# Swapping the order of two kinds of attention scores inside a half step of a four-layer network

## The chip, the cores and the metric

The program runs on one core of a Trainium2 chip. One core has a matrix engine (TensorE, in the profile PE, its weight loads PEld), a vector engine (VectorE, DVE), a scalar engine (ScalarE, ACT), GpSimd (POOL), and SyncE (SP), which here only issues DMAs. Each engine works through its own queue of instructions in order and waits on semaphores for the others. The metric is the device time of one execution in microseconds; lower is better.

## The reference

A network of four layers works on `x` of shape (8, 512, 128). In every layer `x` is normalised, and an attention part and a feed-forward part are added to it:

```python
xn = _layernorm(x, axis=-1)
x = x + _L0_attn_ref(xn, ...) + _L0_ffn_ref(xn, ...)
...
x = x + _L3_attn_ref(xn, ...) + _L3_ffn_ref(xn, ...)
```

Layers 0, 2 and 3 have softmax attention with 16 heads of 8 channels; the change touches only these. Layer 0 masks keys behind the query:

```python
scores = jnp.einsum('bhqd,bhkd->bhqk', qc, k) * scale
causal_mask = k_pos[None, :] > q_pos[:, None]
scores = jnp.where(causal_mask[None, None], -jnp.inf, scores)
...
p = jax.nn.softmax(scores - m, axis=-1)
oc = jnp.einsum('bhqk,bhkd->bhqd', p, v)
```

Layer 2 multiplies the scores by a lower triangular mask and subtracts a million times its complement, and layer 3 adds a bias that depends on the distance of query and key, without a mask. Layer 1 has a linear attention with decay. The feed-forward parts are mixtures of experts of several kinds.

## The kernel before, in words

The three softmax layers share the function `attention`. A unit of work is one batch element `b` and one group `g` of four heads. The scores of a unit are made twice. The straight scores (tile `s`, queries on the partitions) serve only to find the maximum of each row: `first` makes the products (line 297), `first_rest` adds the causal mask as a product with an identity (line 312, layers 0 and 2) and lets VectorE take the maximum (line 318; in layer 3 line 325 besides, for blocks with a near bias). The transposed scores (tile `t`, keys on the partitions) serve for the softmax itself: `second` makes the products (line 366) and adds the negated maximum, which is spread over the partitions by a product with `pick` (line 376, the picks). `second_rest` adds the bias of layer 3 (line 394) or the mask of layer 0 (line 400), and ScalarE takes the exponential (line 404). In layer 2 GpSimd then clears the masked part (line 408). `weigh` multiplies the exponentials with the values (line 421), and `finish` and `divide` complete a unit.

A unit is cut into half steps, 6 in the causal layers and 8 in layer 3. A half step holds two heads of a kind and one or two blocks of keys. The heads of a group lie in the four quarters of 32 rows of the partitions. In half step `x` the straight scores are those of the pair `1 - x % 2` and the transposed ones those of the pair `x % 2`, so that the two kinds use different quarters of the array's rows:

```python
pr = 1 - x % 2                  # first
pr = x % 2                      # second
r = 32 * (2 * pr + k)
```

The straight scores run five units ahead of the transposed ones (`AHEAD`), since the maximum must be known for a whole batch element before it is subtracted. Both kinds, and some tiles of the feed-forward parts, take their place in PSUM from one ring of three buffers:

```python
return ps.tile([P, 2, T], F32, tag="pair", name=name, bufs=3)
```

A buffer comes free when its reader is done: the maximum on VectorE for straight scores, the exponential on ScalarE for transposed ones. Which of the three buffers a tile takes is settled when the program is built.

The function `run` writes out the order of TensorE's queue by hand, inside `tc.manual_schedule`. In each half step it calls `first`, `second`, `first_rest` and `second_rest`, then `now`, which inserts the tasks due at that place (projections, transposes, work of the feed-forward parts), and after every second half step `weigh`. A unit's last block is weighed in the second half step of the unit that follows. The other engines' queues follow from this order and from the builder's own plan.

Of the kernel before, what the change touches and what calls it, by code (L numbers as in the profile page):

```python
# [36 lines left out]
def blk(i, n=P):  # L37
    return slice(i * n, (i + 1) * n)
# [3 lines left out]
def network(ctx: ExitStack, tc: tile.TileContext, io: dict):  # L42
# [11 lines left out]
    def ps_pair(name):  # L54
        return ps.tile([P, 2, T], F32, tag="pair", name=name, bufs=3)
# [12 lines left out]
    x = []  # L68
# [120 lines left out]
    def attention(L, w, causal, scale, bias=None, soft=None, vpad=None, add_masks=False):  # L189
# [9 lines left out]
        st = {}  # L199
# [23 lines left out]
        def spans(x, straight):  # L223

            out, c = [], 0
            for j in pieces[x]:
                n = T - j * P if causal else T
                if straight and (causal or bias is not None):
                    j = NI - 1 - j
                out.append((j, c, n))  # L230
                c += n
            return out, c
# [125 lines left out]
        def second(b, g, x):  # L358

            pr = x % 2  # L360
            q, key, mT = st[b]["q", g], st[b]["k", g], st[b]["mT"]
            s = st["t"] = ps_pair(f"t{L}_{b}_{g}_{x}")
            for k in range(2):
                r = 32 * (2 * pr + k)
                for j, c, n in spans(x, False)[0]:
                    nc.tensor.matmul(  # L366
                        s[:, k, c : c + n],
                        lhsT=key[r : r + 32, blk(j)],
                        rhs=q[r : r + 32, T - n : T],
                        start=(c == 0),  # L370
                        stop=False,
                    )
            for k in range(2):
                r = 32 * (2 * pr + k)
                for j, c, n in spans(x, False)[0]:
                    nc.tensor.matmul(  # L376
                        s[:, k, c : c + n],
                        lhsT=pick[r : r + 32, 2 * pr + k, g : g + 1].to_broadcast([32, P]),
                        rhs=mT[r : r + 32, T - n : T],
                        start=False,  # L380
                        stop=(j == pieces[x][-1] and not add_masks and not (bias is not None and j >= 2)),
                    )

        def second_rest(b, g, x):
            pr = x % 2
            s = st.pop("t")
            blocks, width = spans(x, False)
            if bias is not None and pieces[x][0] >= 2:
                (j,) = pieces[x]
                for k in range(2):  # L390
                    h = g * HG + 2 * pr + k
                    n = 128 * (j - 1)
                    for part in range(2):
                        nc.tensor.matmul(  # L394
                            s[:, k, :n], lhsT=bias[2], rhs=bias[1](h)[part][:, 256 - n :], start=False, stop=part == 1
                        )
            if add_masks:
                for j, c, n in blocks:
                    for k in range(2):
                        nc.tensor.matmul(  # L400
                            s[:, k, c : c + P], lhsT=ident_bf, rhs=mask_kq, start=False, stop=(j == pieces[x][-1])
                        )
            p = wk.tile([P, 2, T], F32, tag="p", name=f"p{L}_{b}_{g}_{x}", bufs=4)
            nc.scalar.activation(p[:, :, :width], s[:, :, :width], AF.Exp, scale=scale)  # L404
            if causal and not add_masks:

                for j, c, n in blocks:
                    nc.gpsimd.affine_select(  # L408
                        p[:, :, c : c + P], p[:, :, c : c + P], pattern=[[0, 2], [1, P]], compare_op=ALU.is_ge,
                        fill=0.0, base=0, channel_multiplier=-1,  # L410
                    )
            for j, c, n in blocks:
                st[b, g, j, pr] = p[:, :, c : c + n]
# [83 lines left out]
    def usual(at, A, start, soft, norms=True):  # L497

        end = A.nh
        for b in range(NB):  # L500
            u = start + 4 * b
            if start + b >= 2:
                at(u - 8, -4, A.begin, b, not norms)
                if norms:
                    at(u - 8, 0, A.normed_turned, b)
                at(u - 8, 2, A.project, b)
                at(u - 4, 3, A.values, b)
                if soft:
                    at(u - 3, 3, A.behind, b)
            if start + b >= 1:  # L510
                at(u - 1, 0, A.maxima, b)
                at(u - 1, 3, A.turn_maxima, b)
            for g in range(NG):
                at(u + g + 1, 2, A.finish, b, g)
                at(u + g + 1, 4, A.divide, b, g)
            at(u + 5, 0, A.end, b)
            at(u + 5, 2, A.add, b)

    def run(layers, tasks, soft, normed=None, begun=0):

        units = [(A, b, g) for A in layers for b in range(NB) for g in range(NG)]
        where = [0]
        for A, _, _ in units:
            where.append(where[-1] + A.nh)
        todo = {}

        def at(u, x, f, *args):

            n = len(units)
            t = (layers[0].nh * u if u < 0 else where[u] if u <= n else where[n] + layers[-1].nh * (u - n)) + x  # L530
            todo.setdefault(t, []).append((f, args))

        for k, A in enumerate(layers):
            usual(at, A, k * NB * NG, soft[k], normed is None)
        tasks(at)
        A = layers[0]

        def now(t):
            for f, args in todo.pop(t, []):
                f(*args)  # L540

        with tc.manual_schedule(engines={mybir.EngineType.PE}):
            for b in range(begun, 2):
                A.begin(b)
                turn_norm(A.L, b, A.st[b]["xn"])
                if normed is not None:
                    normed(b, A.st[b]["xn"])
                A.project(b)
                if b == 0:
                    for g in range(NG):  # L550
                        A.load(0, g)
            for u in range(AHEAD):
                _, b, g = units[u]
                for x in range(A.nh):
                    if x % 2 == 0:
                        pairs = [A.first(b, g, x), A.first(b, g, x + 1)]
                    A.first_rest(b, g, x, pairs[x % 2])
                    if u == 1 and x == 0:
                        A.values(0)
                    if u == 1 and x == 3:  # L560
                        A.values(1)
                    if soft[0] and u in (2, 3) and x == 3:
                        A.behind(u - 2)
                    now((u - AHEAD) * A.nh + x)
                if u < 2:
                    A.load(1, u)
            A.maxima(0)
            A.turn_maxima(0)
            for u, (A, b, g) in enumerate(units):
                F, fb, fg = units[u + AHEAD] if u + AHEAD < len(units) else (None, 0, 0)  # L570
                if u + AHEAD + 1 < len(units):
                    N, nb, ng = units[u + AHEAD + 1]
                    N.load(nb, ng)
                done = 0
                for x in range(A.nh):
                    firsts = []
                    if F:
                        upto = -(-(x + 1) * F.nh // A.nh)
                        firsts, done = range(done, upto), upto
                    for y in firsts[:-1]:  # L580
                        F.first_rest(fb, fg, y, F.first(fb, fg, y))
                    if firsts:
                        s = F.first(fb, fg, firsts[-1])
                    A.second(b, g, x)
                    if firsts:
                        F.first_rest(fb, fg, firsts[-1], s)
                    A.second_rest(b, g, x)
                    now(where[u] + x)
                    back, blocks = A.weights.get(x, (0, ()))
                    if u >= back:  # L590
                        B, wb, wg = units[u - back]
                        for j in B.weights[1][1] if back else blocks:
                            B.weigh(wb, wg, j)
            for j in A.weights[1][1]:
                A.weigh(b, g, j)
            for t in sorted(todo):
                now(t)
# [822 lines left out]
    def more23(at):  # L1420
# [5 lines left out]
        for b in range(NB):  # L1426
# [15 lines left out]
            at(u + 5, 2, store, b)  # L1442

    run([layer2, layer3], more23, [True, False], begun=2)


# [87 lines left out]
```

## Time and profile before

| | |
|---|---|
| median of 3 runs | 2989.63 us (2984.65 to 3001.01) |
| the profiled execution | 2772.28 us, its span 2770.6 us |
| mean granted TensorE clock in it | 0.896 |
| TensorE busy | 2455.6 us, 89% of the span |
| VectorE busy | 1602.8 us, 58% |
| ScalarE busy | 1227.3 us, 44% |
| GpSimd busy | 590.8 us, 21% |

The profiled execution is shorter than the runs without a profile; durations below are those of the profiled one. The four layers follow each other: layer 0 up to about 830 us, layer 1 to about 1580 us, then layers 2 and 3 in one schedule, with layer 3 from about 2200 us.

In the groups of the profile a row gives the line, engine, operation, what is written and read, and the count, then the busy time and the mean duration of one in ns, then the engine's idle time in front of these instructions and what ended most of it. In the timeline a row begins with start and duration. Ends of matrix products are modelled, so starts are the better guide. A row of waits gives the total in us, the number of times and the longest.

### The profile page before, as it was taken

How to read it: one execution, taken by the hardware profiler on the slowest of the kernel's cores; microseconds unless marked ns; L12 is line 12 of the kernel's file. 1: busy time of each engine (PE TensorE's matmuls, PEld its weight loads, DVE VectorE, ACT ScalarE, POOL GpSimd, SP SyncE). 2: the span in 40 equal slices, each digit the busy share in tenths (PEclk: the TensorE clock that was granted, in tenths of full speed). 3: DMA queues.
4: the chain of work that ended last, by engine and by line, in shares of the span. 5: the costliest groups of instructions: out<-in, count | busy, mean ns of one | idle time of the engine just before them, and what ended most of it. 6: DMA issues, size and time to landing. Idle time of an engine off the chain costs nothing.

```text
span 2770.6 us, 45233 instructions
## 1 busy us (share of the span) xinstructions
PE 2455.6 (89%) x17158; PEld 1553.5 (56%) x17158; DVE 1602.8 (58%) x3966; ACT 1227.3 (44%) x1779; POOL 590.8 (21%) x931
## 2 busy tenths in 40 slices
PE   5889988898887899999998788888888899999999
PEld 3555566777773566778886644444443344444444
DVE  8774542222222488756666656666566677777670
ACT  1433456566563333222222044444454455555556
POOL 2027720000005165500002133323332200000000
PEclk6877899999996788999999689889897899999899
DMA  7443346555541221222222322222122111222200
GB/s 221 155 144 124 126 129 180 169 171 165 165 124 39 69 52 48 77 82 80 81 86 61 102 66 67 75 82 65 55 63 63 51 46 58 69 66 65 67 24 10
DMA packets 170792, 252.38 MB, mean 91 GB/s; under 512 B 21712, under 2 KB 94672, under 8 KB 170320
## 3 DMA queue, kind: packets, MB, share of 16 engines
q1 hardware_dynamic: 157904, 221.40, 25.9%
q0 software_dynamic: 12672, 28.10, 3.5%
q8 instruction: 136, 2.23, 0.3%
q14 instruction: 80, 0.66, 0.1%
HBM read 155.57 MB, written 93.85 MB: 90 GB/s over the span
## 4 chain that ended last, share of the span: by engine, by line
PE 39%; DVE 11%; ACT 3%; POOL 2%; issue 2%; DMA 2%; SPq 0%; POOLq 0%; ACTq 0%; DVEq 0%
PE o L421 6%; DVE max L318 6%; PE s L297 4%; PE t L366 3%; PE o L1084 3%; PE rc L1293 3%; PE t L376 2%; PE t L394 2%; PE p L237 2%; PE y L786 2%; PE s L1061 1%; PE h L999 1%; PE h L1001 1%; ACT p L404 1%; DVE sum L325 1%
## 5 line engine op out<-in xcount | busy, mean ns | idle before, releaser
L318 DVE TENSOR_REDUCE max<-s 128x2 f32<-128x1024 f32 (+3 forms) x768 | 664.3, 885 | 376.3 <-PE s L312 268.9
L404 ACT ACTIVATE p<-t 128x1024 f32<-128x1024 f32 (+1 forms) x640 | 596.5, 938 | 548.3 <-PE t L400 195.4
L366 PE MATMUL t<-q,k 32*128 32x512 f32 (+3 forms) x1536 | 326.8, 453 | 109.3 <-ACT p L404 72.4
L297 PE MATMUL s<-k,q 32*128 32x512 f32 (+3 forms) x1536 | 319.0, 452 | 47.4 <-DVE max L318 26.4
L421 PE MATMUL o<-p,vpad 128*32 128x512 f32 (+3 forms) x3072 | 352.2, 547 | 5.0 <-DVE vpad L256 2.5
L800 POOL DMA_INDIRECT yk<-ys_d,slots x160 | 162.0, 1013 | 880.7 <-DMA ys_d<-y 740.0
L297 PEld LDWEIGHTS s<-k,q 32*128 32x128 f32 x1536 | 142.7, 201 | 335.4 <-issue 179.4
L376 PE MATMUL t<-mT,pick 32*128 32x512 f32 (+3 forms) x1536 | 265.8, 371 | 0.0
L366 PEld LDWEIGHTS t<-q,k 32*128 32x128 f32 x1536 | 147.9, 202 | 202.8 <-ACT p L404 101.7
L786 PE MATMUL y<-wt,h 128*128 128x128 f32 x1632 | 202.5, 278 | 17.6 <-DVE xsT L775 11.5
L786 PEld LDWEIGHTS y<-wt,h 128*128 128x128 f32 x1632 | 191.5, 192 | 27.4 <-ACT h L890 10.6
L752 POOL DMA_INDIRECT xs_d<-xr,slots x160 | 157.7, 985 | 160.0 <-DVE slots L744 108.5
L1084 PEld LDWEIGHTS o<-v,a 128*128 128x128 f32 x1280 | 158.7, 199 | 28.0 <-issue 23.8
L888 PE MATMUL h<-xsT,wt 128*128 128x256 f32 x632 | 152.8, 385 | 18.0 <-DVE xsT L775 13.3
L408 POOL TENSOR_SCALAR_AFFINE_SELECT p<-p 128x256 f32<-128x256 f32 x256 | 102.4, 414 | 296.9 <-ACT p L404 295.8
L1084 PE MATMUL o<-v,a 128*128 128x65 f32 x1280 | 163.3, 282 | 1.3 <-DVE a L1071 1.3
L376 PEld LDWEIGHTS t<-mT,pick 32*128 32x128 f32 x1536 | 153.5, 211 | 1.2 <-ACT mT L355 0.9
L890 ACT ACTIVATE h<-h,wt 128x256 f32<-128x256 f32 x316 | 121.8, 478 | 58.7 <-issue 55.5
L421 PEld LDWEIGHTS o<-p,vpad 128*32 128x32 f32 x3072 | 71.3, 114 | 129.7 <-issue 99.9
L888 PEld LDWEIGHTS h<-xsT,wt 128*128 128x128 f32 x632 | 113.8, 190 | 37.7 <-DVE xsT L775 19.2
L312 PE MATMUL s<-mask_qk,ident_bf 128*128 128x128 bf16 x1024 | 133.9, 245 | 0.0
L895 DVE TENSOR_TENSOR y<-y,wt 128x256 f32<-128x256 f32 x79 | 33.5, 424 | 162.4 <-PE y L786 150.7
(271 smaller groups left out, 3655.8 us busy)
## 6 DMA issues: line engine op xcount, KB each, us to landing
wt<-in_f_w SPq DMA_DIRECT2D x79, 578.0 KB, 4.1
q<-apartq SPq DMA_DIRECT2D x96, 256.0 KB, 2.7
k<-apartk SPq DMA_DIRECT2D x96, 256.0 KB, 3.0
wt<-in_f_w SPq DMA_DIRECT2D x23, 768.0 KB, 5.3
xs<-xs_d SPq DMA_DIRECT2D x102, 128.0 KB, 3.3
ys_d<-y SPq DMA_DIRECT2D x102, 128.0 KB, 4.1
xs_d<-zero SPq DMA_DIRECT2D x50, 256.0 KB, 3.9
apartq<-highq SPq DMA_DIRECT2D x48, 256.0 KB, 3.0
```

Source lines behind the costliest of these rows:

```text
L297: nc.tensor.matmul(s[:, j, c : c + n], lhsT=q[r : r + 32, blk(i)], rhs=k[r : r + 32, :n], start=(c == 0), stop=not causal,)
L312: nc.tensor.matmul(s[:, j, c + n - P : c + n], lhsT=ident_bf, rhs=mask_qk, start=False, stop=(i == spans(x, True)[0][-1][0]),)
L318: anchor["vector"] = nc.vector.tensor_reduce(m[:, i, g, 2 * pr : 2 * pr + 2], s[:, :, c : c + n - e], AX.X, ALU.max, negate=True).ins
L366: nc.tensor.matmul(s[:, k, c : c + n], lhsT=key[r : r + 32, blk(j)], rhs=q[r : r + 32, T - n : T], start=(c == 0), stop=False,)
L376: nc.tensor.matmul(s[:, k, c : c + n], lhsT=pick[r : r + 32, 2 * pr + k, g : g + 1].to_broadcast([32, P]), rhs=mT[r : r + 32, T - n : T], ...
L404: nc.scalar.activation(p[:, :, :width], s[:, :, :width], AF.Exp, scale=scale)
L421: nc.tensor.matmul(st[b, g][blk(h, 32), T - n : T], lhsT=vpad[b % 2][:, j, g * HG + h, :], rhs=st[b, g, j, h // 2][:, h % 2, :], start=(j ...
L752: ins = nc.gpsimd.indirect_dma_start(out=xs_d, out_offset=bass.IndirectOffsetOnAxis(ap=slots[:, b * NI + i, k : k + 1], axis=0), in_=state ...
L786: nc.tensor.matmul(py[:, blk(k)], lhsT=h[:, f, blk(k)], rhs=out(wt)[:, f, :], start=(f == 0), stop=(f == 3))
L800: nc.gpsimd.indirect_dma_start(out=yk[:, k, :], out_offset=None, in_=ys_d, in_offset=bass.IndirectOffsetOnAxis(ap=slots[:, b * NI + i, k : ...
L888: nc.tensor.matmul(s[:, f, :], lhsT=wt[:, blk(f)], rhs=xsT, start=True, stop=True)
L1084: nc.tensor.matmul(o[:, k, i * 65 : i * 65 + 65], lhsT=lin[b, c, "a", j][:, k, blk(i - j)], rhs=v1[b % 2][:, j, 2 * c + k, :], start=(j == ...
```

## The change

In `run`, `second` now comes before `first`, and `second_rest` before `first_rest`. The picks of line 376 move from `second` to the start of `second_rest`. So TensorE's order within a half step was straight products, transposed products, picks, mask of the straight scores, bias or mask of the transposed ones; it becomes transposed products, straight products, picks, bias or mask of the transposed scores, mask of the straight ones. The instructions themselves are the same.

```diff
         def second(b, g, x):
 
             pr = x % 2
-            q, key, mT = st[b]["q", g], st[b]["k", g], st[b]["mT"]
+            q, key = st[b]["q", g], st[b]["k", g]
             s = st["t"] = ps_pair(f"t{L}_{b}_{g}_{x}")
...
+
+        def second_rest(b, g, x):
+            pr = x % 2
+            s, mT = st.pop("t"), st[b]["mT"]
+            blocks, width = spans(x, False)
             for k in range(2):
                 r = 32 * (2 * pr + k)
-                for j, c, n in spans(x, False)[0]:
+                for j, c, n in blocks:
                     nc.tensor.matmul(
                         s[:, k, c : c + n],
                         lhsT=pick[r : r + 32, 2 * pr + k, g : g + 1].to_broadcast([32, P]),
...
-
-        def second_rest(b, g, x):
-            pr = x % 2
-            s = st.pop("t")
-            blocks, width = spans(x, False)
...
                     for y in firsts[:-1]:
                         F.first_rest(fb, fg, y, F.first(fb, fg, y))
+                    A.second(b, g, x)
                     if firsts:
                         s = F.first(fb, fg, firsts[-1])
-                    A.second(b, g, x)
+                    A.second_rest(b, g, x)
                     if firsts:
                         F.first_rest(fb, fg, firsts[-1], s)
-                    A.second_rest(b, g, x)
                     now(where[u] + x)
```

## The prediction

> **What bounds the kernel now.** I read the page first (busy shares, clock row, groups), then the busy time by stage, then the waits of the attention stages, then the timeline, half step by half step. From the page:
>
> ```profile
> PE   5889988898887899999998788888888899999999
> ...
> PEclk6877899999996788999999689889897899999899
> ...
> L366 PE MATMUL t<-q,k 32*128 32x512 f32 (+3 forms) x1536 | 326.8, 453 | 109.3 <-ACT p L404 72.4
> L297 PE MATMUL s<-k,q 32*128 32x512 f32 (+3 forms) x1536 | 319.0, 452 | 47.4 <-DVE max L318 26.4
> ...
> L376 PE MATMUL t<-mT,pick 32*128 32x512 f32 (+3 forms) x1536 | 265.8, 371 | 0.0
> ```
>
> TensorE is the bound nearly everywhere, and its queue is in program order, so each microsecond saved on it in attention shortens the run unless another engine's chain ends last. It waits in front of the transposed scores (L366, 109.3 us), less in front of the straight ones (L297, 47.4 us), never in front of the pick products (L376).
>
> Three stages of the run hold half steps with both kinds of scores; layer 1 (about 830 to 1580 us) has none. Columns: busy time by engine with instruction counts, granted clock, DMA share, GB/s.
>
> ```profile
> 130.00:365.00 235.00, 212.31 (x1860) 125.96 (x1858) 135.83 (x299) 94.10 (x122) 129.93 (x134) 0.82 0.41 133
> 1580.00:2190.00 610.00, 521.75 (x3693) 262.75 (x3690) 388.37 (x939) 281.05 (x444) 206.06 (x459) 0.85 0.20 62
> 2190.00:2660.00 470.00, 432.29 (x2820) 202.16 (x2820) 353.55 (x897) 261.12 (x289) 28.78 (x57) 0.95 0.20 62
> ```
>
> VectorE is busy 75% of layer 3 (353.55 of 470) and 64% of layer 2. DMA is far from a limit: this change moves none, and nothing on SP's or POOL's queue changes place. The two shapes of a half step stand side by side in the timeline of layer 0 (start, duration):
>
> ```profile
> 208.81 0.50 PE L297 MATMUL s<-k,q 32*128 32x512 f32 x2
> ...
> 208.82 0.50 PE L366 MATMUL t<-q,k 32*128 32x512 f32 x2
> ...
> 209.16 0.39 PE L376 MATMUL t<-mT,pick 32*128 32x512 f32 x2
> ...
> 209.49 0.29 PE L312 MATMUL s<-mask_qk,ident_bf 128*128 128x128 bf16 x2
> ...
> 209.61 0.28 PE L400 MATMUL t<-mask_kq,ident_bf 128*128 128x128 bf16 x2
> 209.81 1.23 DVE L318 TENSOR_REDUCE max<-s 128x2 f32<-128x1024 f32 x1 [1.31 <-PE s L312]
> ...
> 209.81 0.50 PE L297 MATMUL s<-k,q 32*128 32x512 f32 x2
> 209.98 1.02 ACT L404 ACTIVATE p<-t 128x1024 f32<-128x1024 f32 x1 [1.41 <-PE t L400]
> ...
> 211.06 0.50 PE L366 MATMUL t<-q,k 32*128 32x512 f32 x2 [0.74 <-ACT p L404]
> ...
> 211.40 0.40 PE L376 MATMUL t<-mT,pick 32*128 32x512 f32 x2
> ```
>
> First half step: straight and transposed scores start 0.01 us apart. They use disjoint quarters of the array's rows (one pair of heads in rows 0 to 63, the other in 64 to 127), so the four products run side by side. The picks use the rows of the transposed scores and come 0.34 us later, the next full-height product (L312) 0.33 after that: 0.67 in all. Second half step: the straight scores run alone at 209.81, the transposed ones wait for a buffer until 211.06 (its last reader, the exponential, ended at 211.00), and after that wait the picks still queue 0.34 behind them. I call this split. Counting starts over 0.2 us apart as split, the timeline has 66 split of 159 half steps in layer 0, 82 of 192 in layer 2, 94 of 216 in layer 3. They are mostly the odd half steps; the even ones follow the long `weigh` products.
>
> In layer 3 the releaser is mostly another (total wait, times, longest):
>
> ```profile
> PE t L366 <- DVE max L318: 14.8, 24, 0.9
> PE t L366 <- DVE max L325: 14.2, 30, 0.8
> ...
> PE t L366 <- ACT p L404: 3.3, 3, 1.6
> ```
>
> **The change part by part.** No instruction is added or removed. On TensorE the order S, T, pick, mask S, mask T becomes T, S, pick, mask T, mask S.
>
> 1. The split half step. Whichever kind is second waits, as it takes the buffer freed last. Now S waits, and the picks queued behind it use T's rows, whose products have long streamed. So S and the picks start together, as S and T do at 208.81. From the end of the wait to the next full-height product: 0.34 + 0.33 = 0.67 before, 0.34 after. Saved: 0.33 a split. The new wait in front of S holds up the picks, the masks and `weigh`, and through the picks ScalarE's exponential; the old one in front of T held up the same. A half step that does not wait has T and S together, then picks, as before: 0.
>
> 2. The exponential starts earlier. In layer 0 the mask of T no longer comes behind that of S (209.61 against 209.49): 0.12 us. In a split of layer 2, 0.33 as in step 1. The buffer loop through ScalarE therefore shortens by as much as the TensorE work, so the saving isn't just a longer next wait. For layer 2: before, scores to buffer is 1.9; the pair of half steps is 1.9 + 0.67 + 0.3 (masks) + 1.0 (`weigh`, L421) = 3.9; after, 3.5.
>
> 3. The maximum starts relative to S, not ahead of it. In layers 0 and 2 it waits for mask S, behind the picks either way, so VectorE loses nothing. In layer 3 there is no mask: today S runs early, and VectorE goes from one maximum straight to the next (2407.01 for 1.23, then 2408.22). With S second it starts 0.54 after S (S at 2406.47, maximum at 2407.01). A bare pair takes today 0.67 + 1.0 (`weigh`) to the next S, then 0.54 + 1.23 + 0.04 to the next wait's end: 3.48. If S waits for the maximum before it, both half steps are loops of 0.54 + 1.23 + 0.04: 3.62. If other work stands behind the odd half step, the 0.33 is kept. Bounds for layer 3: 94 x 0.33 = 31 gained, 94 x 0.14 = 13 lost. I take 5 gained: VectorE's 75% is near the losing case.
>
> Sum: layer 0, 66 x (0.33 + 0.12) = 30; layer 2, 82 x 0.33 = 27; layer 3, 5: 62 us.
>
> 4. The clock. In the profile it falls to half for stretches: mean 0.82, 0.85 and 0.95 in the three stages, so half speed for 36%, 30% and 10% of them. The waits before L366 for the exponential are 72.4 us in 74, mean 1.0. The Trainium skill (TensorE: Matmul & The Clock Gate, section Why this matters for your kernels) says to leave no idle gap over about 3 us between bursts; by that rule these short waits cost no clock, the change keeps its 62 us, and the sum would be 2923. By the row, 0.85 in a stage of short waits, they do cost some. The waits stay about as long while the pair shrinks from 3.9 to 3.5: idle share from 0.7/3.9 = 18% to 20%. If half-speed time grows in step, layer 2 gets 3% of 610 = 20 us more of it and layer 0 some 10; at about half of that lost, 14 us. Bounds: 0 by the rule, 60 if the half-speed share doubled in layer 0 and rose by a half in layer 2. I follow the row: 14, and the sum is the one below.
>
> Net: 48 us of the profiled 2772.28 (span 2770.6), so 2724. The runs shown have median 2989.63, 1.078 times that; I scale the gain: 52 us, 2938.
>
> What hides the zero-cost edits: exchanging the two masks costs nothing as both still precede the maximum and the exponential; S's mask comes 0.12 later in layer 0 half steps that are not split, covered by the maximum's 1.2 to 2 us of slack. Without that cover: 93 x 0.12 = 11 us.
>
> **The rivals.**
>
> Slower: VectorE joins the loop. If S, now second, waits for the preceding maximum in every layer (three buffers go round, and which one a tile gets is settled when the program is built), each half step of layer 3 leaves VectorE idle 0.54. A unit of layer 3 takes 18.1 us (the transposes of L353, one in four units, come 72 us apart) with 75% of it, 13.6, VectorE work; 8 x 0.54 = 4.3 more makes 17.9, right at the edge. It decides once VectorE's other idle time exceeds 0.2 us a unit; today all its idle time is 4.5. If half of that stays, a unit takes 20.2: 27 x 2.1 = 57 lost, and layers 0 and 2 gain little, their loop being 1.93 against 1.9. Profiled 2772 + 50, scaled: 3043. For it: the layer 3 waits above. Against: in layers 0 and 2 the exponential ends first and frees the buffer.
>
> No difference: the clock eats it. Half-speed share at 50% in layers 0 and 2 instead of 36 and 30 means some 150 us more at half speed, of which a third to a half is lost: about 55 against 62. Profiled 2765: 2985. For it: the clock flips 72 times already.
>
> No difference: it doesn't do what the order suggests. If the first of the pair, T, is given the late buffer, both start together after the wait and the picks follow as ever: only the mask exchange is left, under 10 us: 2980. Against: the half step before leaves one buffer free a full half step earlier, and the scores placed first take it.
>
> **How the numbers follow.** The net saving, 2938: 0.60. No measurable difference (both rivals): 0.17. VectorE in the loop: 0.23. The runs shown spread by 0.55%, so about 0.5% (15 us) is what a measurement of this kernel can tell from no change. The low end is step 1 everywhere with no clock loss: 30 + 27 + 31 = 88, scaled 95, so 2895; a warmer clock could add a little: 2888. The high end reaches into the slower rival to 3025, short of its full 3043; about 0.1 lies beyond each end. The main case alone: 2895 to 2970.
>
> **What would show it.** Right: in split half steps S comes last and L376 starts within 0.05 us of L297; idle before L366 falls below 40 us and that before L297 rises above 80, released by ACT p in layers 0 and 2; layer 0 to 365 us and layer 2 each shorten by 15 to 30 us, layer 1 not at all. Wrong: L297 waits mostly for DVE max in layers 0 and 2; a unit of layer 3 over 18.5 us with VectorE idle 0.5 before each maximum; a granted clock below 0.80 in layer 2.

## The result, and the profile after

The changed kernel takes 2971.47 us (median of 20 runs, 2953.59 to 2996.56). The kernel before, timed beside it, takes 2993.53 us (20 runs, 2978.27 to 3032.25). The ratio is 0.9929, with a 95% interval of 0.99 to 0.9958: 22 us faster, where 52 were forecast. Here and below, ratios and intervals leave out the runs that are over 1.5% above the fastest of their kernel.

The profile shown ahead of the prediction was taken at 2772 us: against a later profile of the same kernel its layer 0 is 157 us shorter and its layer 1 is 53 shorter, while layers 2 and 3 are alike within 8 us (the last section says what is known of that). So I compare the changed kernel with that later profile, experiment e12, whose span of 2991.8 us is like the timed runs. The changed kernel's span is 2975.1 us.

First the page of the changed kernel: busy tenths, the clock row, and the three groups of score products. The picks are now in line 381.

```profile
PE   5841198889888687689999888888888788888989
...
PEclk6975599999998588799999868888898899998889
...
L297 PE MATMUL s<-k,q 32*128 32x512 f32 (+3 forms) x1536 | 329.4, 462 | 281.8 <-ACT p L404 155.1
...
L366 PE MATMUL t<-q,k 32*128 32x512 f32 (+3 forms) x1536 | 321.9, 447 | 32.6 <-DVE max L318 12.0
...
L381 PE MATMUL t<-mT,pick 32*128 32x512 f32 (+3 forms) x1536 | 289.7, 403 | 1.8 <-issue 1.8
```

The wait has moved as forecast, from the transposed scores (L366, now 32.6 us) to the straight ones (L297). Of the 281.8 us, more than 100 belong to standstills in layer 0, the "11" in the row of busy tenths, which the kernel before has too in this kind of run.

Next the busy time by stage of the changed kernel: layers 0, 2 and 3, in the columns of the prediction's table. I bounded the stages by the transposes of the maxima (L353), which come once for each of the eight batch elements of a layer: layer 0 is here from its first transpose to its sixth, layer 2 from its first to the first of layer 3, and layer 3 to its last. So these bounds differ from the prediction's.

```profile
74.00:529.00 455.00, 265.33 (x2621) 158.94 (x2622) 192.10 (x485) 145.77 (x198) 133.57 (x137) 0.77 0.31 102
1768.00:2355.00 587.00, 498.53 (x3664) 244.34 (x3665) 379.06 (x914) 277.93 (x438) 201.53 (x449) 0.85 0.21 65
2355.00:2902.00 547.00, 481.08 (x3093) 220.67 (x3091) 391.97 (x979) 286.67 (x320) 30.72 (x60) 0.90 0.18 55
```

The same three stages of the kernel before, in e12:

```profile
74.00:566.00 492.00, 304.18 (x2617) 184.97 (x2617) 192.63 (x480) 145.97 (x197) 133.46 (x137) 0.73 0.29 94
1794.00:2396.00 602.00, 520.83 (x3660) 263.21 (x3662) 380.38 (x914) 277.44 (x437) 202.62 (x452) 0.84 0.20 63
2396.00:2919.00 523.00, 482.68 (x3099) 225.40 (x3098) 385.77 (x983) 288.51 (x320) 30.72 (x60) 0.93 0.19 57
```

Layer 0 is 37 us shorter, layer 2 is 15 shorter, layer 3 is 24 longer. The rest of layer 0 took 445 us before and 444 after. Layer 1, which has no such half steps, took 784 us in e12 and 795 after: 11 longer. The sum is -17 us, and the spans differ by 16.7. So the question is layer 3: TensorE is busy as long as before (481 against 483 us), and the stage is 24 us longer all the same, at a granted clock of 0.90 instead of 0.93.

### The profile page after: what moved, and what is told of

It is laid out like the page before. It is cut to its first block, busy times and chain, and to the rows that moved or that the text cites. A ratio compares the mean times of both kernels' runs of the same rounds, so it can differ in the third digit from the quotient of the medians.

```text
span 2975.1 us, 45259 instructions
## 1 busy us (share of the span) xinstructions
PE 2425.7 (82%) x17158; PEld 1517.0 (51%) x17158; DVE 1605.7 (54%) x3966; ACT 1225.9 (41%) x1779; POOL 588.7 (20%) x931
## 4 chain that ended last, share of the span: by engine, by line
PE 44%; DVE 12%; ACT 5%; issue 3%; another core or an unknown queue 2%; POOL 2%; DMA 1%; SPq 0%; ACTq 0%; DVEq 0%; POOLq 0%
PE o L421 7%; DVE max L318 5%; PE t L366 4%; PE o L1084 4%; PE s L297 3%; PE rc L1293 3%; PE s L1061 2%; PE t L394 2%; PE y L786 2%; PE qk L1032 2%; PE t L381 2%; PE h L999 1%; PE h L1001 1%; ACT p L404 1%
## 5 line engine op out<-in xcount | busy, mean ns | idle before, releaser
L318 DVE TENSOR_REDUCE max<-s 128x2 f32<-128x1024 f32 (+3 forms) x768 | 667.0, 886 | 508.2 <-PE s L312 234.5
L297 PE MATMUL s<-k,q 32*128 32x512 f32 (+3 forms) x1536 | 329.4, 462 | 281.8 <-ACT p L404 155.1
L421 PE MATMUL o<-p,vpad 128*32 128x512 f32 (+3 forms) x3072 | 364.3, 558 | 18.9 <-issue 14.8
L366 PE MATMUL t<-q,k 32*128 32x512 f32 (+3 forms) x1536 | 321.9, 447 | 32.6 <-DVE max L318 12.0
L297 PEld LDWEIGHTS s<-k,q 32*128 32x128 f32 x1536 | 147.5, 204 | 363.0 <-ACT p L404 181.0
L366 PEld LDWEIGHTS t<-q,k 32*128 32x128 f32 x1536 | 143.4, 198 | 348.1 <-issue 182.2
L381 PE MATMUL t<-mT,pick 32*128 32x512 f32 (+3 forms) x1536 | 289.7, 403 | 1.8 <-issue 1.8
L888 PEld LDWEIGHTS h<-xsT,wt 128*128 128x128 f32 x632 | 113.8, 190 | 38.9 <-DVE xsT L775 19.6
L1071 DVE TENSOR_TENSOR a<-s,decay 128x1024 f32<-128x1024 f32 (+3 forms) x128 | 100.0, 815 | 39.1 <-PE s L1061 25.0
```

What stands on the lines that cost most here:

```text
L297: nc.tensor.matmul(s[:, j, c : c + n], lhsT=q[r : r + 32, blk(i)], rhs=k[r : r + 32, :n], start=(c == 0), stop=not causal,)
L318: anchor["vector"] = nc.vector.tensor_reduce(m[:, i, g, 2 * pr : 2 * pr + 2], s[:, :, c : c + n - e], AX.X, ALU.max, negate=True).ins
L366: nc.tensor.matmul(s[:, k, c : c + n], lhsT=key[r : r + 32, blk(j)], rhs=q[r : r + 32, T - n : T], start=(c == 0), stop=False,)
L381: nc.tensor.matmul(s[:, k, c : c + n], lhsT=pick[r : r + 32, 2 * pr + k, g : g + 1].to_broadcast([32, P]), rhs=mT[r : r + 32, T - n : T], ...
L421: nc.tensor.matmul(st[b, g][blk(h, 32), T - n : T], lhsT=vpad[b % 2][:, j, g * HG + h, :], rhs=st[b, g, j, h // 2][:, h % 2, :], start=(j ...
L888: nc.tensor.matmul(s[:, f, :], lhsT=wt[:, blk(f)], rhs=xsT, start=True, stop=True)
```

## The experiments

For all of them the picks are a function of their own, and a list `NEW` says which layers have the new order. `NEW = ()` gives the program of before, and all three layers give the changed one.

```diff
+    NEW = ()                       # or (0,), (0, 2), (3,), (0, 2, 3)
...
+                    if A.L in NEW:
+                        A.second(b, g, x)
                     if firsts:
                         s = F.first(fb, fg, firsts[-1])
-                    A.second(b, g, x)
+                    if A.L not in NEW:
+                        A.second(b, g, x)
+                    A.picks(b, g, x)
+                    if A.L in NEW:
+                        A.second_rest(b, g, x)
                     if firsts:
                         F.first_rest(fb, fg, firsts[-1], s)
-                    A.second_rest(b, g, x)
+                    if A.L not in NEW:
+                        A.second_rest(b, g, x)
```

My theory was that in layer 3 the straight scores, now second, wait for the maximum before them and so hold up the next one, a loop through VectorE. The rivals: a colder clock, with the waits only beside it; an order that is dearer for TensorE itself; and a gain that is small in every layer, with no loss anywhere.

The experiments ran in three sessions, each with its own runs of the kernel before. That kernel's median was 2763.06 us in the first session (27 runs), 3002.97 in the second (30) and 3004.01 in the third (11). The first and the third were on the same chip, so the level belongs to the session. Ratios are taken within a session.

### e1: the order of before, in every layer

```diff
+    NEW = ()
```

> The kernel before, unchanged, for a second profile. The profile of before showed a span of 2770.6 us while its runs are near 2990, and the profile after (2975.1) holds engines that stand still for about 115 us in layer 0 (190 to 360 us) while GpSimd scatters rows, and 65 us more in layer 1. If that standstill belongs to the program and not to the new order, this profile is near 2980, and has the same standstill in layers 0 and 1, with layers 2 and 3 (from the ninth transposing of the maxima on) at 1115 +- 20 us. If the new order causes it, this profile is near 2775 again.

Measured: one run of 2779.47 us, among the 2747.35 to 2783.91 of the kernel before. Its profile (span 2777.8) is my profile of before for the first session: layer 0 343 us, layer 1 720, layer 2 606, layer 3 518.

### e2 and e3: the new order in layers 0 and 2, and in layer 3

```diff
-    NEW = ()
+    NEW = (0, 2)                   # e3: (3,)
```

> The new order only in half steps whose transposed scores belong to layers 0 and 2, the old one in layer 3. Theory A (layer 3 gives the gain back, since its straight scores now wait for the preceding maximum and VectorE stands in the loop): 40 to 55 us faster than before, ratio 0.982 to 0.987, so better than the whole change. Theory B (the half-speed clock eats the gain everywhere): ratio 0.992 to 0.996, like the whole change. Theory C (the standstill beside the scatter absorbs what layer 0 saves): 15 to 25 us from layer 2 alone, 0.991 to 0.995.

> The new order only in layer 3. Theory A: 15 to 35 us slower than before, ratio 1.005 to 1.012, VectorE idle about 0.5 us in front of each maximum, L297 waiting mostly for DVE max. Theory B: within 0.3% of before.

Measured: e2 2740.19 us, ratio 0.9919 (0.9892 to 0.9945); e3 2796.1 us, ratio 1.0144 (1.011 to 1.0178). So the change is two changes of opposite sign: 23 us gained in layers 0 and 2 (less than my theory's 40 to 55, and in the band of theory C), 33 lost in layer 3. Layer 3 by stage, first e3, then e1, then e2, where layer 3 has the old order:

```profile
2157.00:2707.00 550.00, 487.03 (x3097) 224.75 (x3097) 391.34 (x981) 287.77 (x321) 30.80 (x60) 0.88 0.17 55
```

```profile
2187.00:2705.00 518.00, 476.83 (x3095) 223.12 (x3094) 384.97 (x980) 288.11 (x320) 30.74 (x60) 0.94 0.19 58
```

```profile
2154.00:2695.00 541.00, 503.08 (x3096) 233.93 (x3095) 386.60 (x982) 288.78 (x321) 30.81 (x60) 0.88 0.18 55
```

Against e1 the stage grew by 32 us and TensorE's busy time by 10; the other 22 are waits. But the clock differs too. e2 and e3 have the same clock, 0.88, and there the new order costs 9 us (550 against 541). So of the 32 us about 9 are there at equal clock, and the rest goes with a colder one. That a profile of the old order is as cold shows that a single profile can mislead; the timed runs decide. They are slower in e3 by 33 us, and their median granted clock is 0.892, against 0.899 for the kernel before and 0.907 in e2. So with the new order in layer 3 the clock is colder in the runs as well.

What the waits are, the changed kernel shows in its timeline of layer 3 (start, duration; in brackets the idle time before and its releaser):

```profile
2691.28 0.50 PE L366 MATMUL t<-q,k 32*128 32x512 f32 x2
...
2692.36 0.08 DVE L325 DVE_READ_ACCUMULATOR2_ANT max<- 128x1 f32 x1
...
2692.59 0.50 PE L297 MATMUL s<-k,q 32*128 32x512 f32 x2 [0.80 <-DVE max L325]
...
2692.59 0.50 PE L381 MATMUL t<-mT,pick 32*128 32x512 f32 x2
...
2693.03 0.33 PE L394 MATMUL t<-far_high,far_rest 128*128 128x128 f32 x1
...
2693.12 0.96 DVE L318 TENSOR_REDUCE max<-s 128x2 f32<-128x768 f32 x1 [0.19 <-PE s L297]
...
2694.61 0.50 PE L366 MATMUL t<-q,k 32*128 32x512 f32 x2
2694.79 0.08 DVE L325 DVE_READ_ACCUMULATOR2_ANT max<- 128x1 f32 x1
...
2695.02 0.50 PE L297 MATMUL s<-k,q 32*128 32x512 f32 x2
...
2695.03 0.50 PE L381 MATMUL t<-mT,pick 32*128 32x512 f32 x2
```

Straight scores and picks start together, as step 1 said. But the straight scores now wait for the maximum before them, and the next maximum waits for those scores: maximum ends at 2692.44, scores start at 2692.59, next maximum at 2693.12. VectorE works to 2694.87, scores start at 2695.02, and (in the rows that follow) the next maximum at 2695.55. From one maximum to the next are 2.43 us; 1.75 is VectorE's work, and 0.68 is the way through TensorE and back. The second of these half steps comes after `weigh`, the kind that did not wait before.

The waits of layer 3, total, times and longest. The changed kernel:

```profile
PE s L297 <- DVE max L318: 29.6, 30, 1.7
PE s L297 <- DVE max L325: 22.5, 32, 2.1
...
PE t L366 <- ACT p L404: 9.7, 7, 1.4
```

The kernel before, e12:

```profile
PE t L366 <- DVE max L318: 15.4, 24, 1.2
PE t L366 <- DVE max L325: 13.3, 27, 0.8
...
PE s L297 <- DVE max L318: 7.6, 7, 1.1
```

Waits for the maximum, 36.3 us on the three rows of before, became 52.1 on the first two of after, and they now stand in front of the scores that VectorE needs next. All waits in front of the two kinds of scores together went from 38.9 to 63.7 us, as much more as the stage is longer. TensorE's busy time stays level because two things offset each other in it: the split half steps got shorter, and the clock is colder. In e6, further down, where the clock is 0.93 again, it is 460 us.

### e4: the new order in layer 0 alone

```diff
-    NEW = ()
+    NEW = (0,)
```

> The new order only in layer 0. Theory A: 20 to 30 us faster, ratio 0.990 to 0.993. Theory C: under 8 us, ratio over 0.997. Theory B: 5 to 15 us faster with a granted clock lower than before in the stage from 75 to 500 us.

Measured: 2753.73 us, the median of 22 runs, 9 under the kernel before. The ratio, 0.9921 (0.9894 to 0.9948), rests on 13 of the 22 and would make it 22 us; as the runs are spread evenly from 2721 to 2778 us, I trust the 9 more. By stage, layer 0 took 327 us in its profile, 343 in e1 and 335 in e3. With e2's 23 this leaves 14 for layer 2. In layer 0 more was gained and given back. The fifth of the six transposes that bound the stage came 337 us into the span in e1, 328 in e3, and 296 in e2 and e4, so 32 to 41 us earlier; but from there to the sixth took 80 to 81 us with the old order and 104 to 105 in e2 and e4, where TensorE, VectorE and ScalarE stand still together for 26 and 28 us. I put that down to the rows for the experts, which wait for the end of the 128 scatters of POOL, and the change does not move these. That became the theory that e8 tests.

### e5 and e6: the whole change, and the whole change with the buffers in rotation

e5 is the changed kernel again (`NEW = (0, 2, 3)`). e6 gives the three buffers in strict turn (passing over one that a state of layer 1 holds), so that in a pair T always takes the one and S the next, and S always follows a transposed tile, whose reader is the exponential:

```diff
-        return ps.tile([P, 2, T], F32, tag="pair", name=name, bufs=3)
+        turn_of[0] += 1
+        while turn_of[0] % 3 == held[0]:
+            turn_of[0] += 1
+        return ps.tile([P, 2, T], F32, tag=f"pair{turn_of[0] % 3}", name=name, bufs=1)
```

> The whole change beside runs of before on one chip. The runs of before came out near 2990 where the result was measured and near 2763 beside the first four experiments. If the parts add up as measured there (layer 0 -9, layer 2 -14, layer 3 +40): where before takes 2763, this takes 2775 to 2790, ratio 1.004 to 1.010, so slower; where before takes 2990, ratio 0.990 to 0.996 as recorded, since the scatter's end no longer holds back what layer 0 saves. The rival, that parts don't add up: 0.993 in both.

> The whole change, with the three score buffers taken in plain rotation in place of the builder's choice (skipping the one that layer 1 holds). In layer 3 the straight scores then take the buffer of the transposed scores before them (freed by the exponential) and not that of the straight scores before them (freed by the maximum). Theory A (the loss in layer 3 is the straight scores waiting for the preceding maximum): layer 3 (nine transposes of maxima from the end to the last) falls from 548 to 500 to 520 us, L297 waits for ACT, not DVE max. Rival (layer 3 loses to the half-speed clock or to VectorE's late start whichever buffer is taken): 540 to 560 us. Layers 0 and 2 within 5 us of the whole change; layer 1 unknown, read by itself.

Measured: e5 2977.82 us, ratio 0.9911 (0.9883 to 0.9939); e6 2986.76 us, ratio 0.9925 (0.99 to 0.995). The two intervals overlap: the rotation gains nothing as a whole. Layer 3 took 543 us in e5 and 530 in e6. Its busy row and its main wait in e6 (line 302 is 297 there, 414 the exponential):

```profile
2365.00:2895.00 530.00, 460.44 (x3096) 211.19 (x3095) 388.95 (x980) 288.34 (x321) 30.73 (x60) 0.93 0.18 57
```

```profile
PE s L302 <- ACT p L414: 57.4, 77, 1.7
```

The maximum is gone from in front of the straight scores, and the stage lies between the two forecasts: 530 us, against 543 in e5 and 523 in e12. But the waits are no shorter: 57.4 us for the exponential in place of 52.1 for the maximum. What came back is TensorE's busy time, 460 us against 478 in e5, with a clock of 0.93 again. At that clock, that of e12, the new order still costs 7 us, about as much as between e3 and e2. Layer 2, which gained 15 us with the change as it is, took 601 us in e6, about as before. So this choice of buffers only changed which reader is late.

### e7 and e8: layer 0 without its scatters

Both leave out the 128 scatters of layer 0, so its experts work on rows of zeros.

```diff
-            for i in range(NI):
-                at(6, 4 + 8 * b + 2 * i, m["scatter"], b, i)
```

e7 has the old order everywhere, e8 has `NEW = (0,)`.

> The old order, without the 128 scatters of layer 0 (the experts there then work on rows of zeros; as many blocks, same shapes). Theory C (the experts' first block waits for the scatter's end at 365 us): layer 0 up to the first expert block 0 to 10 us shorter than in the old order with scatters; and where before takes 2990, 100 us and more shorter, the standstill being tied to the scatters.

> The same without scatters, with the new order in layer 0. Theory C: 25 to 35 us faster than the old order without scatters, against 9 us with them, as the half steps between the fourth batch and the experts no longer give 24 us back. Rival (the end of layer 0 is bound by TensorE's tasks): still 9 us.

Measured: e7 2840.16 us (2830.08 to 2850.1), e8 2801.52 us (2795.07 to 2810.01). The new order in layer 0 is worth 39 us without the scatters, a little more than the 25 to 35 expected. Layer 0 in e7, then in e8:

```profile
74.00:416.00 342.00, 306.22 (x2613) 188.46 (x2613) 192.35 (x479) 145.57 (x196) 6.08 (x6) 0.81 0.34 109
```

```profile
74.00:379.00 305.00, 269.98 (x2618) 162.61 (x2617) 191.34 (x476) 145.90 (x197) 6.09 (x6) 0.88 0.38 122
```

37 us shorter, and the last stretch that had grown to 104 us is 74 here. So in the first session the scatters held back a good part of layer 0's gain. The granted clock rose from 0.81 to 0.88 with the new order, where I had expected it to fall; TensorE's busy time fell by 36 us for the same instructions.

### e9 and e10: a shorter maximum in layer 3

Both let the maximum of layer 3 read 256 columns of each head instead of up to 512, and leave out the maximum over the blocks with a near bias. The maxima are then those of part of the keys.

```diff
-                    m[:, i, g, 2 * pr : 2 * pr + 2], s[:, :, c : c + n - e], AX.X, ALU.max, negate=True
+                    m[:, i, g, 2 * pr : 2 * pr + 2], s[:, :, c : c + (256 if L == 3 else n - e)], AX.X, ALU.max, negate=True
...
-                for j in range(2 if e else 0):
+                for j in range(0):
```

e9 has the old order, e10 the new one in layer 3.

> The old order, with the maximum of layer 3 taken over 256 columns of each head only and without the second instruction for the near bias (so the maxima are not the true ones): VectorE has about 0.4 us of work on a half step in place of 1.2 to 1.8. The base for the next run. Layer 3 (ninth-last to last transposing of the maxima) 470 to 500 us against 515 to 518.

> The same short maximum, new order in layer 3 alone. Theory A (the loss in layer 3 is the late start of the maximum, whose 1.2 to 1.8 us then stand in the loop): with the short maximum nothing is lost, ratio to the old order with the short maximum 0.995 to 1.003 (layer 3 within 8 us), and L297 no longer waits for DVE max. Rival (the new order costs TensorE itself or the clock, whatever VectorE does): again 30 to 40 us slower, ratio 1.010 to 1.015.

Measured: e9 2927.66 us, ratio 0.9757 (0.9687 to 0.9827); e10 2913.38 us, ratio 0.972 (0.9655 to 0.9784). Layer 3 in e9, then in e10:

```profile
2378.00:2847.00 469.00, 446.30 (x3097) 208.71 (x3095) 224.46 (x534) 286.57 (x320) 30.81 (x60) 0.96 0.21 64
```

```profile
2380.00:2837.00 457.00, 424.93 (x3098) 197.94 (x3096) 225.28 (x533) 284.46 (x319) 30.97 (x61) 0.97 0.21 66
```

VectorE falls from 386 us of work to 225, and the same order that cost 21 to 33 us in layer 3 costs nothing: the stage is 12 us shorter, and the median 14 lower, though the two intervals overlap. The clock does not fall either (0.96 and 0.97). So the loss of layer 3, the colder clock included, needs VectorE's load. An exchange of order that is itself dear for TensorE, or a cost of the picks in their new place, would have shown here too. One part of the expectation failed: the straight scores of e10 still wait for the maximum.

```profile
PE s L297 <- DVE max L318: 22.1, 29, 1.4
```

Waits for the maximum in front of both kinds of scores are 16.7 us in e9 and 26.1 in e10. But few half steps are split in either, 38 in e9 and 36 in e10, and the stage does not get longer.

### e11 and e12: layers 0 and 2 again, and before

e11 is the program of e2, e12 that of before, in the third session.

> The new order in layers 0 and 2, the old in layer 3, once more. Where before takes about 2990: layer 0 -37 (as without the scatter), layer 2 -14, so 45 to 55 us faster, ratio 0.981 to 0.986, and faster than the whole change. Where before takes about 2763: as in the first run of it, 0.992.

> The kernel before once more for its profile. If before takes about 2990 on this chip: layer 0 from the first to the sixth transposing of the maxima takes 490 to 510 us (455 and 469 in the two profiles of the whole change), layer 1 780 to 800, layers 2 and 3 as in the other profiles of before; instruction loads all but stop while the scatters of layer 0 run. If it takes 2763: 335 to 345, as before.

Measured: e11 2941.61 us (2935.18 to 2953.89), ratio 0.9813 (0.9769 to 0.9857); e12 one run of 2993.53 us, whose profile is shown above. e11 beats the kernel before in both sessions in which it ran (0.9919 in the first), and it beats the whole change: the intervals of the whole change in this kind of session, 0.99 to 0.9958 and e5's 0.9883 to 0.9939, lie above it. The median granted clock of its runs is 0.876, against 0.865 for the kernel before. Layer 3 in e11:

```profile
2343.00:2867.00 524.00, 483.97 (x3100) 224.94 (x3096) 386.26 (x981) 288.34 (x320) 31.19 (x62) 0.93 0.19 57
```

Layer 3 is back at 524 us, e12's 523; layer 0 took 451 us and layer 2 590.

## Why the prediction was right or wrong

The prediction failed in layer 3: in step 3, and in the sentence of step 1 that it rests on. It had 5 us gained there and 13 lost at worst; 21 to 33 were lost. In the profiles that is 29 of the some 31 us between the 48 forecast and the 17 measured. Layer 1, put at nothing, lost 11, and layers 0 and 2 together gained 10 more than forecast, for a reason that the prediction had the other way round. The sizes, in us. The last column takes the stages of the changed kernel, e5 and e11 against e12, and for the first session the stages and times of e2, e3 and e4 against e1 and the kernel before:

| term | forecast | measured |
|---|---|---|
| a split half step | -0.33 | -0.22 |
| layer 0 | -30 | -23 to -41; -8 to -22 in the first session |
| layer 2 | -27 | -10 to -15; -14 to -23 in the first session |
| layer 3 | -5 | +21 to +33 |
| clock, layers 0 and 2 | +14 | a gain in layer 0, none clear in layer 2; both are in the rows above |
| layer 1 | 0 | +2 to +11 |

**Step 1, the size.** After the wait, straight scores and picks start at the same time, and the next full-height product follows 0.44 us later (2692.59 to 2693.03 above), not 0.34. I took 0.34, the time between the scores and the picks when they use the same rows, for the time from four products side by side to a full-height one. Over all split half steps at full clock, the median from the later start to the next full-height product went from 0.66 to 0.44 us in each of the three layers: 0.22 saved, not 0.33. Layer 2 has 71 to 80 split half steps in either order, depending on the profile and on how they are paired; 78 x 0.22 = 17 us is near the 10 to 15 and 14 to 23 that the stage shows.

**Step 1, the sentence that failed.** "A half step that does not wait has T and S together, then picks, as before: 0." This holds only while the same half steps wait. In layer 3 they did not stay the same: with a gap of over 0.2 us counted as split, 93 of 218 half steps were split in e12 and 134 in the changed kernel, and the mean gap grew from 0.76 to 0.83 us. Half steps behind `weigh`, which had started both kinds together, now wait as well.

**Step 3, the sign.** The step named the cause, the 0.54 us from the straight scores to the maximum, and set it for the odd half steps at +0.14 against -0.33 a pair. Its bounds, 31 gained and 13 lost, were too narrow on the side of loss: they let only those half steps lose that waited already. The loop closes at 134 half steps, and the timeline has 0.68 us of VectorE's idle time in one. A unit of layer 3 (28 of them in the stage) takes 523/28 = 18.7 us in e12 and 547/28 = 19.5 after. VectorE's idle time before L318 rose from 96.4 to 111.3 us over 218 and 219 maxima, from 0.44 to 0.51 each. The marks that I had set for "wrong" are met but do not tell the orders apart: e12 is over 18.5 us a unit already, and e2, with the old order and the clock at 0.88, has 112.0 us of that idle time. e9 and e10 do tell: VectorE's work on the scores decides. The step also left out the clock, which the prediction priced in layers 0 and 2 alone. The larger part of the loss came with a colder clock: 9 of e3's 32 us are there at the clock of e2, and 7 in e6 at that of e12.

**The slower rival** had the mechanism, in one layer of three. It priced layer 3 at 57 us lost, about twice what was measured, with a unit of 20.2 us, and without the clock. In layers 0 and 2 it fails for the reason given against it: the straight scores wait for the exponential there. In the changed kernel's layer 2 the longest row of waits in front of L297 is

```profile
PE s L297 <- ACT p L404: 35.6, 32, 2.5
```

The maximum loses nothing in those layers, since it waits for the mask behind the picks in either order, as step 3 said.

**Step 2 and layer 0.** Step 2's 0.12 is there. At full clock, the median from the later of the two score starts to the exponential went from 1.16 us in e7 to 0.82 in e8 in split half steps, and from 1.16 to 1.04 in the others. So a split saves 0.34, not 0.45, and 66 x 0.34 = 22 us. e5, whose clock in this stage is that of e12 (0.73), is 23 us shorter than e12, and TensorE is busy 22 us less:

```profile
73.00:542.00 469.00, 282.08 (x2621) 168.55 (x2621) 192.64 (x479) 146.33 (x197) 133.74 (x137) 0.73 0.30 99
```

The 37 us of the changed kernel and the 41 of e11 come with a clock of 0.77, and the 37 of e8 with 0.88 against 0.81. So that the measured 37 lie near the forecast 30 is partly luck: the steps give about 22, and the rest came with a warmer clock. I had also taken the scatters for other work beside the path. In the first session their end was the next thing late, and only part of the 32 to 41 us was left.

**Step 4, the clock.** The row 0.85 led me to take 14 us off for a colder clock. In layer 2 the granted clock went from 0.84 to 0.85, and in layer 0, where the scatters do not disturb it, from 0.81 to 0.88; over whole runs it rose in e2 and e11. So the rival that the clock eats the gain of layers 0 and 2 is out. (Its gain of 7 us in 2772 scales to 2982, not 2985; nothing hangs on it.) The rule that I weighed against the row (the Trainium skill, TensorE: Matmul & The Clock Gate, section Why this matters for your kernels) gave 0 for waits this short, and 0 was nearer. It does not carry to layer 3, where waits of at most 2.1 us went with a fall from 0.93 to 0.90. Whether the new waits caused that fall is not shown, since e2 has such a clock with the old order; e10 shows only that without VectorE's load there is none.

**The rival of the late buffer for T** is out: L366 waits 32.6 us in all, and S starts with the picks.

**What stays open.** Why layer 1 is 11 us longer, no run shows: in this kind of session it took 790 to 795 us in the profiles of the whole change (the changed kernel, e5 and e6) and 779 to 787 in the others. The whole change was not timed in a session of the first kind. Its parts, timed there, multiply to 0.9919 x 1.0144 = 1.006, a small loss. That the same change gains 0.7% at 2990 us and may lose 0.6% at 2763 rests on that product alone.

## What to carry to other kernels

When two tiles share a ring of buffers, the one placed second gets the wait, so put second the tile whose reader has slack: ask for each stage which reader is busy, and whether its next work starts with the tile that you delay. A change that saves time only where work already waits needs a count of where it will wait afterwards, since the new order makes its own waits. Where one schedule serves several stages, time the edit stage by stage: here the same edit gained in two layers and lost in the third, and with it left out of the third (e11) the gain was 1.9% instead of 0.7 to 0.9%. And compare such stages at equal granted clock before reading a few us: of the 32 us of e3 in layer 3, only 9 were left.

## What the hardware did that I had not expected

**Standstills beside the scatters.** In the second and third sessions (except in e7 and e8, without scatters) and in the changed kernel's profile, TensorE, VectorE and ScalarE together stand still for 8 to 33 us at a time (52 once in e6) in layer 0 while POOL issues its 128 scatters. The waits of the changed kernel between 190 and 360 us, "remote" standing for a releaser that the profile doesn't show:

```profile
DVE max L318 <- remote: 133.2, 6, 33.5
ACT p L404 <- remote: 128.5, 6, 37.3
```

In the first session the same program on the same chip (e1) has none of it. The DMA queues from 190 to 400 us, e12 first and e1 second (packets, MB, share of the DMA engines):

```profile
q0 software_dynamic: 4576, 9.97, 12.6%
q1 hardware_dynamic: 2446, 5.37, 8.3%
q8 instruction: 3, 0.05, 0.1%
```

```profile
q1 hardware_dynamic: 8766, 15.62, 24.2%
q0 software_dynamic: 4576, 9.97, 13.8%
q8 instruction: 12, 0.20, 0.4%
```

The scatters run at the same pace in both. In e12 the other two queues hardly move beside them, though the DMA engines are idle four fifths of the time, and only 3 loads of instructions arrive instead of 12. Over the whole of layer 0 both have 21 such loads, so they come late, not fewer. Leaving the scatters out (e7) takes 163 us off the median. So the scatters are a necessary part of the standstills, though not of all that differs between the sessions: layer 1 takes 787 us in e7 too, against 720 in e1. That the engines stand for want of instructions fits these rows, but no run isolates it, and what differs between the sessions I don't know. The Trainium skill (Runtime: NRT & Kernel Launch, section Instruction fetch mechanics) calls the cost of such loads mostly hidden; if they are the cause, it is not hidden in e12.

**Four side-by-side products are not as cheap as two.** From the start of straight scores with picks to the next full-height product are 0.44 us; one kind behind the other on the same rows takes 0.34 for the first and 0.33 for the second.
